# Four quarter-array products in place of four half-array products in one gate of a graph GRU

## The chip, the cores and the metric

The kernel runs on one core of a Trainium2 chip. The metric is the device time of one execution in microseconds (us), as a median over runs. A core has five engines that run their own queues of instructions side by side and wait for one another by semaphores: TensorE (PE in the profile; its weight loads are listed as PEld), VectorE (DVE), ScalarE (ACT), GpSimd (POOL) and SyncE (SP), which here only issues DMA transfers. TensorE reads its operands from SBUF, the on-chip memory of 128 partitions, and writes sums into PSUM, which has eight banks; VectorE and ScalarE read them from there.

## The reference, cut to what matters

There are N = 3327 nodes with 64 features and a dense weighted adjacency matrix `adj` in f32, symmetric in its zeros but not in its weights. Four layers are added to `x`, each on a normalised copy `h`:

```python
def _ggc(x, adj, W, wih, whh, bih, bhh):          # one GRU cell over the graph
    m = adj @ (x @ W)
    gi = m @ wih.T + bih
    gh = x @ whh.T + bhh
    i_r, i_z, i_n = jnp.split(gi, 3, axis=-1)
    h_r, h_z, h_n = jnp.split(gh, 3, axis=-1)
    r = jax.nn.sigmoid(i_r + h_r)
    z = jax.nn.sigmoid(i_z + h_z)
    n = jnp.tanh(i_n + r * h_n)                   # the new value
    return (1.0 - z) * n + z * x

h = relu(layernorm(x));  x = x + relu(_ggc(relu(_ggc(h, ...W1...)), ...W2...))   # layer 0: two cells
# layer 1: adj's non-zeros, ranked and weighted by powers of 1/2, times h @ weight
# layer 2: three products with adj * adj and linear layers;  layer 3: two products with adj, tanh
```

In the gates r and z the input's and the state's sums are only ever needed added together. In the new value n they are needed apart: `h_n` (the state's sum) is first multiplied by r, and then `i_n` (the input's sum) is added.

## The kernel before, in words

**Data.** The nodes are padded to 26 blocks of 128, in two halves of 13 blocks, `s` = 0 and 1. A chunk is a run of 3 or 4 blocks taken from both halves at once: chunks 0, 1 and 2 have 3 blocks (384 columns), chunk 3 has 4 (512 columns). `GROUPS` pairs them: chunks 0 and 1 are group 0, chunks 2 and 3 group 1.

**Products with adj.** There are eight of them, k = 0 to 7; k = 0 and 1 belong to the two GRU cells, k = 2 to the ranked layer. Line L697 (`propagate`) issues them: for a source block and a chunk, one product for each half `s`, each with 128 rows and 64 columns of the array, the first on the left half of the columns and the second on the right half. Their result for a chunk lies in one PSUM bank, half 0 in partitions 0 to 63 and half 1 in partitions 64 to 127. All other products of the kernel have the same 128-by-64 form, and where an operand has only 64 rows, its other half is filled with zeros.

**The GRU cell.** When the sums of a chunk are complete, `after_0` or `after_1` runs `gru`. Its input lies in `both[c]`, 128 partitions by two halves: for each half `s`, the chunk's state is in one half of the partitions and the sums (L942 by ScalarE, then L946 by VectorE in the second cell) are copied into the other. The tile `cells[:, cell, s, g, :]` holds the weights of gate g: g = 0 and 1 are r and z with the input's and the state's weights on top of each other, g = 2 has the state's weights of n in one half of the rows and zeros in the other, g = 3 the input's weights of n in the opposite half of the rows. So `gate(g)` (L1007) is two products, one for each `s`, and gates 2 and 3 multiply 64 of their 128 rows by zeros. In the first cell gate 2 is done ahead of time (`ahead_of_cell`, L217); in the second cell all four gates follow one another. Then ScalarE takes the sigmoids of r and z (L1012), VectorE forms (`nh` + bias) * r (L1017) and adds `ni` (L1019), ScalarE takes the tanh (L1028), and VectorE finishes the cell (L1032 to L1034).

**Order.** Everything is put into the engines' queues in an order fixed at build time. `run` goes through a list of units (one source block for one chunk), and after each unit `spend` advances the tasks that the `yield` statements cut into pieces, by an estimated time. `take` and `give` hand out the eight PSUM banks (`sum` 0 to 3, `temp` 0 to 3). Each engine then works off its own queue, held up only by semaphores.

**What lies around the change.** The second cell runs for chunk 2 at 149.5 us, for chunk 3 at 160.4, for chunk 0 at 200.5 and for chunk 1 at 206.0 (starts of the first gate). Between these VectorE makes masks for the later layers (L509 and L512 for counting, L517 for the ranked layer). From chunk 0's cell on, products of the ranked layer are mixed in: L326 multiplies a mask by a triangular matrix, L575 (ScalarE) or L573 (VectorE) turns the sums into weights, and L697 uses them.

Of the kernel before, what the change touches and what calls it, by code (L numbers as in the profile page):

```python
# [96 lines left out]
def upper(n):  # L97
    return slice(n * D, (n + 1) * D)
# [3 lines left out]
def kernel(  # L102
# [9 lines left out]
    nc = tc.nc  # L112
# [16 lines left out]
    cells = const.tile([P, 2, 2, 4, D], F32, name="cells")  # L129
# [3 lines left out]
    both = [const.tile([P, 2, (b1 - b0) * P], F32, name=f"both{c}") for c, (b0, b1) in enumerate(CH[:NC])]  # L133
# [184 lines left out]
    def width(c):  # L318
        return blocks(c) * P
# [15 lines left out]
    def take(sums=False, either=True):  # L335


        either = either and not sums
        pool = idle_sums if sums else idle_temps
        if either and idle_sums and (not pool or released[idle_sums[0]] < released[pool[0]]):  # L340
            pool = idle_sums
        for c in list(tasks):
            if not pool and c not in running:
                advance(c)
        i = pool.popleft()
        return i, banks[i]

    def give(i):
        released[i] = max(released) + 1
        (idle_sums if i < 4 else idle_temps).append(i)  # L350

    def nodes(c):

        return feat.tile([P, blocks(c), 2, D], F32, name=f"y{c}")
# [17 lines left out]
    def advance(c):  # L372
        running.add(c)
        try:
            tasks[c][1] = next(tasks[c][0])
        except StopIteration:
            del tasks[c]
        running.discard(c)
# [562 lines left out]
    def evacuate_stacked(acc, c, on_scalar=False):  # L941
        nc.scalar.copy(both[c][upper(0), 0], acc[0][1][upper(0), :width(c)])  # L942
        if on_scalar:
            nc.scalar.copy(both[c][upper(1), 1], acc[1][1][upper(1), :width(c)])
        else:
            nc.vector.tensor_copy(both[c][upper(1), 1], acc[1][1][upper(1), :width(c)])  # L946
        for i in {acc[0][0], acc[1][0]}:
            give(i)
# [39 lines left out]
    def turn(yk, c, s):  # L988

        v = both[c][upper(1 - s), s].rearrange("p (b q n) -> p b q n", q=4, n=32)  # L990
        for f in range(2):
            for q in range(4):
                nc.vector.transpose(yk[q * 32:(q + 1) * 32, :, s, f * 32:(f + 1) * 32], v[f * 32:(f + 1) * 32, :, q])

    def gru(acc, c, bi, bh, cell, pace=1.0):

        assert cell in have
        w = width(c)
        evacuate_stacked(acc, c, on_scalar=cell == 0)
        yield 0.8 * pace  # L1000
        at = dead.popleft()
        r, z, d = (slots[at].rearrange("p s w -> p (s w)")[:, i * CWM:i * CWM + w] for i in range(3))

        def gate(g):
            i, ps = take()
            for s in range(2):
                nc.tensor.matmul(ps[upper(1 - s), :w], cells[:, cell, s, g, :], both[c][:, s], start=True, stop=True)  # L1007
            return i, ps

        for g, v in enumerate((r, z)):  # L1010
            i, ps = gate(g)
            nc.scalar.activation(v, ps[:, :w], AF.Sigmoid, bias=bsum[:, cell, g:g + 1])  # L1012
            give(i)
        nh = None if cell == 0 else gate(2)
        ni = gate(3)
        yield 0.75 * pace
        nc.vector.scalar_tensor_tensor(r, ahead[c] if nh is None else nh[1][:, :w], bcol[:, bh + 2:bh + 3], r,  # L1017
                                       op0=ALU.add, op1=ALU.mult)
        nc.vector.tensor_tensor(r, r, ni[1][:, :w], ALU.add)  # L1019
        give(ni[0])  # L1020
        if nh is not None:
            give(nh[0])
        else:
            del ahead[c]
            if not any(ch in ahead for ch in GROUPS[c // 2]):
                rooms[c // 2].free()
        yield 1.2 * pace
        nc.scalar.activation(r, r, AF.Tanh, bias=bcol[:, bi + 2:bi + 3])  # L1028
        yield 0.8 * pace
        for s in range(2):  # L1030
            u = upper(1 - s)
            nc.vector.tensor_tensor(d[u], both[c][u, s], r[u], ALU.subtract)  # L1032
        nc.vector.tensor_tensor(d, d, z, ALU.mult)
        nc.vector.tensor_tensor(d, d, r, ALU.add)  # L1034
        if cell == 0:
            nc.vector.tensor_scalar(both[c][upper(0), 1], d[upper(0)], 0.0, None, op0=ALU.max)
            if c in GROUPS[1]:
                turned[c] = nodes(c)
                turn(turned[c], c, 1)
        yield 2.4 * pace  # L1040
        if cell == 0:
            nc.scalar.activation(both[c][upper(1), 0], d[upper(1)], AF.Relu)
            yield 0.6 * pace
        return at, d
# [27 lines left out]
    def after_0(c, acc):  # L1072
        at, _ = yield from gru(acc, c, BI1, BH1, 0)
        dead.append(at)
        if c in GROUPS[0]:
            yk = nodes(c)
            i, v = stacked_to_nodes(c, lambda s: ident[:, upper(1 - s)])
            yield 0.96
            nc.vector.tensor_copy(flat(yk), v)
            give(i)  # L1080
        else:
            yk = turned.pop(c)
            turn(yk, c, 0)
        y[1][c] = yk

    def after_1(c, acc):
        pace = 1.0 if c in GROUPS[0] else 0.9
        at, h2T = yield from gru(acc, c, BI2, BH2, 1, pace)
        v = transpose_to_nodes(h2T, c)
        dead.append(at)  # L1090
        yield 2.05 * pace
        residual(v, c, relu=True)
        yk = nodes(c)
        yield from layernorm_relu(yk, c, TWO27, 1.2 * pace, squares_on_scalar=c in GROUPS[1])
        y[2][c] = yield from in_three(yk, c)
        yield 80.0 if c in GROUPS[1] else 14.0
        assert "row" in have
        add_row(c, 3)
# [127 lines left out]
```

## Time and profile before

| | |
|---|---|
| median of 3 runs | 685.08 us (684.77 to 685.13) |
| profiled execution | 684.89 us |
| its span in the trace | 683.2 us |
| granted TensorE clock | 1.0 throughout |
| TensorE products issued | 4984 passes, 672.1 us busy |
| VectorE, ScalarE busy | 390.5 us, 272.4 us |
| DMA from the adjacency matrix | 199.08 MB, mean 295 GB/s over the span |

The profile is of one execution. Its span begins with the first and ends with the last recorded instruction, so 1.7 us of the execution's own time lie outside it. An f32 product appears as two TensorE records, one for each of two passes, and each pass has a weight load of its own. The end of a TensorE record is modelled and includes the pipe behind the array, so consecutive records overlap; the distance from one start to the next is what a pass costs in a stream. "128*64" in a row stands for 128 rows and 64 columns of the array. A time in square brackets is how long the engine was idle before that row, with the instruction that released it.

### The profile page before, as it was taken

The page shows a single profiled execution, that of the slowest core. Times are in us where ns is not written, and L with a number is a line of the kernel's source. Part 1 is how long each engine was busy: PE and PEld are TensorE (multiplying, and loading weights), DVE is VectorE, ACT ScalarE, POOL GpSimd, SP SyncE. Part 2 cuts the span into 40 slices and gives each one's busy share as a digit, 9 for nine tenths or more (in the row PEclk, how much of TensorE's full clock was granted, in tenths as well). Part 3 has the DMA queues.
Part 4 walks back from the last instruction along what each step waited for, and adds up shares of the span by engine and source line. Part 5 has one row for each costly group of instructions (what it writes and reads, how often), then busy time and mean ns, then how long its engine had stood idle before and what let it go on. Part 6 is the DMA issues. An engine that isn't in the chain of part 4 may idle for free.

```text
span 683.2 us, 12502 instructions
## 1 busy us (share of the span) xinstructions
PE 672.1 (98%) x4984; PEld 369.8 (54%) x4984; DVE 390.5 (57%) x839; ACT 272.4 (40%) x427; POOL 76.9 (11%) x115
## 2 busy tenths in 40 slices
PE   7999999999999999999999999999999999999997
PEld 5776444445558886566455554444444443344464
DVE  7954898739998999666542108215483893005101
ACT  1014000312148988999987009522366510000101
POOL 5400000002660504021000000000010000000000
PEclk9999999999999999999999999999999999999999
DMA  9999998299889615783999379954997399918991
GB/s 340 401 401 405 405 405 308 78 344 399 279 270 339 244 56 164 274 307 119 358 400 324 124 281 406 406 231 141 401 375 252 123 408 404 405 46 313 397 404 45
DMA packets 68693, 201.30 MB, mean 295 GB/s; under 512 B 7244, under 2 KB 8372, under 8 KB 68636
## 3 DMA queue, kind: packets, MB, share of 16 engines
q1 hardware_dynamic: 65724, 199.08, 78.0%
q10 hardware_dynamic: 736, 1.23, 0.5%
q8 instruction: 39, 0.64, 0.4%
q0 software_dynamic: 2176, 0.20, 0.2%
q14 instruction: 18, 0.15, 0.1%
HBM read 199.45 MB, written 0.85 MB: 293 GB/s over the span
## 4 chain that ended last, share of the span: by engine, by line
PE 94%; DVE 2%; POOL 2%; issue 0%; DMA 0%; ACT 0%; DVEq 0%; ACTq 0%; POOLq 0%
PE sum L697 81%; PE temp L326 5%; PE temp L1007 2%; PE sum L326 1%; PE temp L598 1%; PE sum L1007 1%; PE temp L886 1%; PE temp L611 1%; POOL both L256 1%; DVE e L573 0%; POOL st L966 0%; DMA xs<-in_x 0%; DVE adj L517 0%; DVE st L963 0%; DVE y L962 0%
## 5 line engine op out<-in xcount | busy, mean ns | idle before, releaser
L697 PE MATMUL sum<-adj,y 128*64 128x384 f32 (+3 forms) x3016 | 533.0, 501 | 0.0
L697 PEld LDWEIGHTS sum<-adj,y 128*64 128x64 f32 x3016 | 242.7, 137 | 241.4 <-issue 151.3
L481 ACT ACTIVATE adj<-adj 128x768 f32<-128x768 f32 (+1 forms) x169 | 138.1, 890 | 27.0 <-DMA adj<-in_adjT 13.7
L517 DVE TENSOR_SCALAR adj<-adj 128x768 f16<-128x768 f32 (+2 forms) x156 | 86.2, 594 | 9.8 <-DMA adj<-in_adjT 6.7
L697 PE MATMUL sum<-e,both 128*64 128x384 bf16 (+1 forms) x624 | 73.9, 339 | 0.0
L575 ACT ACTIVATE e<-temp,bitsb 128x384 int16<-128x384 f32 (+1 forms) x113 | 63.6, 605 | 13.2 <-PE temp L326 11.3
L942 ACT COPY both<-sum 64x384 f32<-64x384 f32 (+3 forms) x17 | 8.1, 478 | 145.4 <-PE sum L697 145.3
L483 DVE TENSOR_TENSOR adj<-adj 128x768 f32<-128x768 f32 (+1 forms) x39 | 37.7, 1013 | 42.9 <-DMA adj<-in_adjT 31.8
L946 DVE COPY both<-sum 64x384 f32<-64x384 f32 (+3 forms) x11 | 6.2, 561 | 97.9 <-ACT both L942 96.7
L937 DVE STREAM_TRANSPOSE y<-t 32x96 f32<-32x96 f32 (+1 forms) x128 | 35.6, 278 | 40.8 <-ACT t L922 39.2
L966 POOL TENSOR_TENSOR st<-st,mhalf 128x6 f32<-128x6 f32 (+1 forms) x16 | 25.5, 1592 | 296.9 <-DVE st L964 296.9
L697 PEld LDWEIGHTS <-both 128*64 128x64 bf16 x624 | 44.6, 110 | 13.3 <-issue 3.5
L523 POOL DMA_DIRECT2D adj<-totals x52 | 32.0, 617 | 165.4 <-DVE adj L512 128.6
L326 PE MATMUL temp<-adj,tri 128*64 128x384 bf16 (+1 forms) x316 | 49.0, 341 | 0.1
L573 DVE TENSOR_SCALAR e<-temp 128x384 int16<-128x384 f32 (+1 forms) x45 | 27.7, 618 | 19.1 <-ACT e L575 12.0
L326 PEld LDWEIGHTS <-tri 128*64 128x64 bf16 x416 | 30.3, 110 | 13.7 <-issue 7.8
L915 DVE STREAM_TRANSPOSE both<-y 32x96 f32<-32x96 f32 (+1 forms) x128 | 35.6, 278 | 2.5
L512 DVE SCALAR_TENSOR_TENSOR adj<-adj,adj 128x896 f16<-128x896 f32 x26 | 28.4, 1092 | 0.9
L922 ACT ACTIVATE t<-sum,hopcol 128x384 f32<-128x384 f32 (+1 forms) x8 | 4.9, 608 | 51.8 <-PE sum L697 49.0
L575 ACT ACTIVATE e<-sum,bitsb 128x384 int16<-128x384 f32 (+1 forms) x35 | 20.5, 593 | 5.4 <-PE sum L326 3.8
L598 PE MATMUL temp<-adj,behind 128*64 128x384 f16 x104 | 18.4, 327 | 2.1 <-DVE adj L517 1.9
L326 PE MATMUL sum<-adj,tri 128*64 128x384 bf16 (+1 forms) x100 | 18.5, 335 | 0.9 <-DVE e L573 0.7
(153 smaller groups left out, 360.0 us busy)
## 6 DMA issues: line engine op xcount, KB each, us to landing
adj<-in_adjT SPq DMA_DIRECT2D x130, 768.0 KB, 8.7
adj<-in_adjT SPq DMA_DIRECT2D x104, 896.0 KB, 12.9
xs<-in_x ACTq DMA_DIRECT2D x1, 448.0 KB
adj<-totals POOLq DMA_DIRECT2D x26, 3.0 KB, 4.6
adj<-totals POOLq DMA_DIRECT2D x26, 3.5 KB, 2.9
out<-xs ACTq DMA_DIRECT2D x1, 256.0 KB
xs<-in_x ACTq DMA_DIRECT2D x1, 192.0 KB, 3.1
xs<-in_x SPq DMA_DIRECT2D x1, 192.0 KB
```

Of the source, the lines that this page charges most:

```text
L326: nc.tensor.matmul(out[hs], lhsT[:, hs], rhs, start=start, stop=stop)
L481: nc.scalar.activation(sq, v, AF.Square)
L483: nc.vector.tensor_tensor(sq, v, v, ALU.mult)
L512: nc.vector.scalar_tensor_tensor(t.mask.ones, t.view()[:, 1], 0.0, t.mask.ones, op0=ALU.not_equal, op1=ALU.add)
L517: nc.vector.tensor_scalar(to[:rows, half], t.view()[:rows, half], 0.0, None, op0=ALU.not_equal)
L523: nc.gpsimd.dma_start(out=t.mask.view[P - 1:P], in_=totals[t.g][t.q:t.q + D + 1:D, :])
L573: nc.vector.tensor_scalar(wide[:, s], ps[:, :w], BITS, 0.0, op0=ALU.add, op1=ALU.max)
L575: nc.scalar.activation(wide[:, s], ps[:, :w], AF.Relu, bias=bitsb)
L697: nc.tensor.matmul(acc[h][1][h * D:(h + 1) * D, :w], yq[h], rhs[h], start=first and n == 0, stop=last and n == len(terms) - 1)
L915: nc.vector.transpose(to[at:at + 32, :, q], h[q * 32:(q + 1) * 32, :, s, f * 32:(f + 1) * 32])
L937: nc.vector.transpose(yk[q * 32:(q + 1) * 32, :, s, f * 32:(f + 1) * 32], v[at:at + 32, :, q])
L966: nc.gpsimd.tensor_tensor(st[:, 3, :n], st[:, 2, :n], mhalf[:, :n], ALU.pow)
```

## The change

In the second cell, gates 2 and 3 are no longer two calls of `gate`. Both PSUM banks are taken first, and then four products are issued, each with only the 64 rows that hold weights. For each half `s` of the nodes one product is the state's, into the bank `nh`, and one the input's, into `ni`. The two use opposite halves of the rows and the same half of the columns, so that the four products lie in the four quarters of the array. The zeros are not multiplied any more. The first cell keeps its form; only its two lines are written differently.

```diff
             i, ps = gate(g)
             nc.scalar.activation(v, ps[:, :w], AF.Sigmoid, bias=bsum[:, cell, g:g + 1])
             give(i)
-        nh = None if cell == 0 else gate(2)
-        ni = gate(3)
+        if cell == 0:
+            nh, ni = None, gate(3)
+        else:
+            nh, ni = take(), take()
+            for s in range(2):
+                for (_, ps), g, rows in ((nh, 2, upper(1 - s)), (ni, 3, upper(s))):
+                    nc.tensor.matmul(ps[upper(1 - s), :w], cells[rows, cell, s, g, :], both[c][rows, s],
+                                     start=True, stop=True)
         yield 0.75 * pace
```

`upper(n)` is the slice of partitions from 64 n to 64 n + 63. The issue order before was: state's sum for `s` = 0, state's for `s` = 1, input's for 0, input's for 1. It is now: state's for 0, input's for 0, state's for 1, input's for 1. The banks, the number of products, passes and weight loads, and the order on all other engines stay as they were; the wait for the bank of `ni` moves from the third product to the second.

## The prediction

> **What bounds the kernel now.** I read the page first: its busy times and the chain that ended last.
>
> ```profile
> PE 672.1 (98%) x4984; PEld 369.8 (54%) x4984; DVE 390.5 (57%) x839; ACT 272.4 (40%) x427; POOL 76.9 (11%) x115
> ...
> PE 94%; DVE 2%; POOL 2%; issue 0%; DMA 0%; ACT 0%; DVEq 0%; ACTq 0%; POOLq 0%
> ```
>
> TensorE is busy for 98% of the span and holds 94% of the chain, so over the whole kernel its time is the end. But the change sits in four places only, the second cell's gates of chunks 2, 3, 0 and 1 (near 150, 161, 201 and 207 us), and there the question is which wait ends last. So next came the gate line L1007 and the timeline of weight loads at chunk 0.
>
> ```profile
> L1007 PE MATMUL temp<-both,cells x72: 486/486/592, 60.8 to 208.3; 128*64 128x384 f32 x56, 128*64 128x512 f32 x16
> ```
>
> ```profile
> 200.52 0.20 PEld L1007 LDWEIGHTS sum<-both,cells 128*64 128x64 f32 x4 [0.62 <-DVE both L946]
> 200.90 0.14 PEld L1007 LDWEIGHTS temp<-both,cells 128*64 128x64 f32 x2 [0.18 <-ACT e L575]
> ...
> 201.87 0.14 PEld L1007 LDWEIGHTS temp<-both,cells 128*64 128x64 f32 x2 [0.18 <-issue]
> 202.19 0.14 PEld L1007 LDWEIGHTS temp<-both,cells 128*64 128x64 f32 x2 [0.18 <-ACT adj L1012]
> 202.51 0.14 PEld L1007 LDWEIGHTS temp<-both,cells 128*64 128x64 f32 x2 [0.18 <-issue]
> ```
>
> Each f32 product is two passes, and the two halves of the columns run side by side: a pair of weight loads every 0.32 us. A pass of 384 columns thus costs 0.322 us of stream, though its record says 0.486: the other 0.164 us is the pipe behind it, which the next pass covers. A product of 384 columns is 0.645 us, one of 512 columns 0.86 us (the chain gives 0.86 us to its four passes). The gates begin at 200.52 because they waited for VectorE's copy at L946. That sent me to VectorE.
>
> ```profile
> 152.40 0.62 DVE L1017 SCALAR_TENSOR_TENSOR adj<-sum,bcol,adj 128x384 f32<-128x384 f32 x1 [2.31 <-PE sum L1007]
> ...
> 153.83 0.63 DVE L509 TENSOR_SCALAR adj<-adj 128x896 f16<-128x896 f32 x1 [0.16 <-PE sum L697]
> ```
>
> ```profile
> 159.69 0.69 DVE L946 COPY both<-sum 64x512 f32<-64x512 f32 x1 [0.25 <-ACT both L942]
> ```
>
> ```profile
> 199.91 0.56 DVE L946 COPY both<-sum 64x384 f32<-64x384 f32 x1
> ...
> 202.81 0.62 DVE L1017 SCALAR_TENSOR_TENSOR adj<-temp,bcol,adj 128x384 f32<-128x384 f32 x1 [1.28 <-PE temp L1007]
> ```
>
> ```profile
> 159.70:200.40 40.70, 40.70 (x316) 23.63 (x312) 39.94 (x83) 9.41 (x20) 25.34 (x37) 1.00 0.88 305
> ```
>
> The last line is a stretch with busy times of TensorE, weight loads, VectorE, ScalarE and GpSimd: VectorE works 39.94 of 40.70 us. From 159.69 to 201.53 it waits for nobody, and between 152.40 and 159.69 it has only two short waits (0.16 and 0.25 us). TensorE and VectorE are tied here within tenths of a microsecond.
>
> **Part 1, what is removed.** Four products of 128 rows, two on each half of the columns one after the other, become four of 64 rows, which can run side by side. Pass and load counts stay. If they do run side by side, one product time goes per chunk: 3 x 0.645 + 0.86 = 2.79 us, 0.41% of the time. That is the ceiling.
>
> **Part 2, what is added: two changes of the array's division per chunk**, into quarters and back. Every TensorE row of before is 128*64, so no row shows one. From below: nothing (a change from fp16 to f32 operands, L634 to L697 at 199.73, leaves no gap), and not below nothing, since no pass gets shorter by it. From above: the pipe empties and the weights load in the open, 0.164 + 0.05 = 0.21 us; the 0.05 is what the restart at 200.52 lost (0.37 us to the next pass instead of 0.32). I take 0.21, since a restart from an empty pipe is the row that it is nearest to. Net gain on TensorE: 0.645 - 0.43 = 0.215 us in a chunk of 384 columns, 0.43 in chunk 3.
>
> The Trainium skill says in TensorEngine Tiling (Array Packing), Key Properties, that changing the tiling mode drains TensorE; it gives no price, and no run here shows one yet. By that rule the sum is the one with 0.21 us; without it, the one of the first rival.
>
> **Part 3, when VectorE gets its operands.** L1017 reads the state's sum (`nh`). In the new order its second half is the third product, which now starts with the others: it ends one change, 0.21 us, later than before. The input's sum (`ni`) is ready some 0.4 us earlier, but L1019 runs after L1017 and never waited for it.
>
> **Part 4, what reaches the end.** Chunk 2: L1017 starts 0.21 us later, and the wait of 0.16 us at L509 shrinks by about 0.12, so VectorE is free at 159.53 instead of 159.44. The accumulator is done 0.215 us earlier, so ScalarE's L942 ends at 159.45 instead of 159.66. L946 moves from 159.69 to about 159.55. Chunk 3: the gates start some 0.1 us earlier, `nh` comes 0.21 us later than that, so L1017 (163.36 before) starts 0 to 0.1 us later. From there VectorE is packed to 200.47, so chunk 0's gates start where they did, at 200.5: what TensorE gained in chunks 2 and 3 (0.65 us) becomes idle time before L946.
>
> Chunk 0: 0.215 us, and this passes on. L326 after the gates comes earlier, ScalarE's L575 follows (it was idle 0.9 us before), then L942 and L946 of chunk 1, and VectorE has 1.0 us free before that L946 (204.98 to 206.00), which covers the later L1017. Chunk 1: 0.215 us again; what follows (L575 at 209.68, the tanh at L1028, L573 at 212.22) is released by TensorE, with ScalarE 0.9 us idle before. The other edits cost nothing: the `ni` bank is claimed 0.645 us earlier, but the only waiting one, chunk 0's, hangs on ScalarE's L635, which ends at 201.52, before the quarters begin at 201.87.
>
> Sum: 684.89 (span 683.2 and 1.7 around it) - 0.43 = 684.46 for the profiled execution, which lies 0.19 below the median of 685.08. So 684.6 as a median, 0.07% faster. About 0.2% (1.37 us) is what a measurement of this kernel can tell from no change, so this reads as the same. With changes of 0.05 to 0.35 us each, this case runs from 683.7 to 685.4.
>
> **Rival 1, free changes.** If the array re-divides between two passes, each chunk keeps 0.645 us. VectorE is then not delayed at L1017, and gives back about 0.36 us of its two short waits, which also reaches chunk 0: 0.36 + 2 x 0.645 = 1.65, so 683.4. For it: the change of operand type costs nothing. Against: nothing shows rows re-divided. Even here the gain of chunk 3 is lost in the packed VectorE.
>
> **Rival 2, slower: the row halves take turns.** Nothing in the trace shows two products sharing a half of the columns at once. If they take turns, nothing is removed and both changes are paid: 0.43 us lost per chunk. Chunk 2 then delays L946 by 0.43; chunk 3's `nh` comes 0.43 + 0.21 late, so packed VectorE brings chunk 0 some 0.7 us late, and chunks 0 and 1 add 0.43 each: 1.55 us, 686.6. With side-by-side quarters TensorE itself loses from 0.32 us per change; changes of 0.5 us, no row of which I have, would give 1.4 us or more the same way, by late `nh` (a small case, 686.5 and up).
>
> **Rival 3, slower: products start strictly in program order.** Then a product's second pass holds back the next one's first, and four products take five passes, 1.61 + 0.43 against 1.29 us: 0.75 lost, 0.86 in chunk 3. `nh` is late by 0.86 and 1.07, VectorE brings 1.8 us to chunk 0, two times 0.75 follow: 3.3 us, 688.4. The timeline at chunk 2 speaks against it:
>
> ```profile
> 151.53 0.49 PE L1007 MATMUL temp<-both,cells 128*64 128x384 f32 x1
> ...
> 151.81 0.49 PE L1007 MATMUL sum<-both,cells 128*64 128x384 f32 x1
> ```
>
> There sum is gate 2 and temp gate 3. A pass of gate 3 starts at 151.53, ahead of gate 2's last at 151.81, on the other half of the columns. So halves are not held to one order; that quarters aren't either is a step beyond. The Trainium skill, in TensorE: Matmul & The Clock Gate, part 3, says that matmuls start and end strictly in order; by that rule it would be this rival, and the two rows disagree with it.
>
> **How the numbers follow.** Side by side with paid changes 0.50 (684.6); free changes 0.20 (683.4); turns 0.17 (686.6); dear changes 0.06; program order 0.07 (688.4). Faster by over 0.2% is the second case, 0.20; same the first, 0.50; slower the other three, 0.30. The range goes from 683.2, just below the free case, to 687.0, above the turns; it leaves out program order and the dearest changes.
>
> **What would show it.** In the trace after, the four quarters' first passes at chunk 0 should start within some 0.05 us of each other, about 0.2 us after the last pass of gate 1 has left its stream, and the next line's first pass about 1.07 us after that stream's end instead of 1.29. VectorE's wait at L1017 of chunk 2 should grow by 0.2 us, and TensorE's wait for L946 at chunk 0 by some 0.6 us. It is wrong if pass starts in the quarters are 0.32 us apart, if chunk 0's gates start more than 0.3 us away from 200.5, or if a wait appears that isn't at these four places.

## The result and the profile after

| | before | changed |
|---|---|---|
| median of 18 runs each, us | 684.97 (684.69 to 685.23) | 683.76 (683.62 to 684.35) |
| profiled execution, us | 684.89 | 683.78 |
| its span, us | 683.2 | 682.1 |

The ratio is 0.9983 (0.9977 to 0.999): 1.21 us or 0.17% faster. That is still inside the 0.2% taken as the bound of "the same", but the interval lies wholly below 1. The new median lies between the forecast (684.6) and the first rival (683.4).

The page of the changed kernel, busy times and chain:

```profile
PE 670.8 (98%) x4984; PEld 363.7 (53%) x4984; DVE 389.4 (57%) x839; ACT 272.4 (40%) x427; POOL 77.7 (11%) x115
...
PE 93%; DVE 3%; POOL 2%; issue 1%; ACT 0%; DMA 0%; DVEq 0%; ACTq 0%; POOLq 0%
```

The numbers of instructions are those of before; TensorE's busy time fell by 1.3 us. The quarters are line L1020. This row has its 20 passes into the `temp` banks; 12 more, of the same form, go into `sum` banks:

```profile
L1020 PE MATMUL temp<-both,cells x20: 482/533/640, 151.7 to 207.7; 64*64 64x384 f32 x16, 64*64 64x512 f32 x4
```

**Do the quarters run side by side?** The timeline of TensorE's passes at chunk 2, in the changed kernel:

```profile
151.71 0.53 PE L1020 MATMUL sum<-both,cells 64*64 64x384 f32 x1
151.72 0.53 PE L1020 MATMUL temp<-both,cells 64*64 64x384 f32 x1
151.72 0.53 PE L1020 MATMUL sum<-both,cells 64*64 64x384 f32 x1
151.73 0.53 PE L1020 MATMUL temp<-both,cells 64*64 64x384 f32 x1
152.08 0.48 PE L1020 MATMUL sum<-both,cells 64*64 64x384 f32 x1
152.09 0.48 PE L1020 MATMUL temp<-both,cells 64*64 64x384 f32 x1
```

Yes: four products start their first passes within 0.02 us, and their second passes follow 0.37 us later, again together.

**What does a change of the division cost?** The same engine at chunk 0:

```profile
200.81 0.81 PE L1007 MATMUL temp<-both,cells 128*64 128x384 f32 x4
201.55 0.88 PE L1020 MATMUL temp<-both,cells 64*64 64x384 f32 x8
202.36 0.35 PE L326 MATMUL temp<-adj,tri 128*64 128x384 bf16 x2
202.54 0.33 PE L326 MATMUL sum<-adj,tri 128*64 128x384 bf16 x2
```

Gate 1's records end at 201.62; without the pipe of 0.164 us its stream ends at 201.456. The quarters begin at 201.55, so 0.09 us later, and their first pass takes 0.37 us instead of 0.322, since its weights load in the open: 0.14 us. On the way back, the stream ends at 202.43 - 0.164 = 202.266, L326 begins at 202.36, again 0.09 us later, and the first pair is 0.02 us longer than the next (0.35 against 0.33; 0.05 us where the next line is f32, as at chunk 2). So a change costs 0.11 to 0.14 us, not 0.21. From gate 1's stream to the next line it is 0.90 us, where before had 1.29 and the prediction 1.07. With the 0.02 us of the longer first pair, 1.29 - 0.92 = 0.37 us is what TensorE saves in this chunk.

**Who waits for it?** VectorE in the changed kernel, in three stretches of its timeline (L1023 is what was L1017, L1025 was L1019):

```profile
152.71 0.62 DVE L1023 SCALAR_TENSOR_TENSOR adj<-sum,bcol,adj 128x384 f32<-128x384 f32 x1 [2.48 <-PE temp L1020]
...
153.90 0.62 DVE L509 TENSOR_SCALAR adj<-adj 128x896 f16<-128x896 f32 x1
...
158.55 1.09 DVE L512 SCALAR_TENSOR_TENSOR adj<-adj,adj 128x896 f16<-128x896 f32 x1
159.67 0.69 DVE L946 COPY both<-sum 64x512 f32<-64x512 f32 x1
```

```profile
163.58 0.75 DVE L1023 SCALAR_TENSOR_TENSOR adj<-temp,bcol,adj 128x512 f32<-128x512 f32 x1 [0.18 <-PE sum L1020]
164.44 0.69 DVE L1025 TENSOR_TENSOR adj<-adj,sum 128x512 f32<-128x512 f32 x1
165.04 1.96 DVE L517 TENSOR_SCALAR adj<-adj 127x768 bf16<-127x768 f32 x4
```

```profile
199.50 0.56 DVE L946 COPY both<-sum 64x384 f32<-64x384 f32 x1
...
202.56 0.62 DVE L1023 SCALAR_TENSOR_TENSOR adj<-temp,bcol,adj 128x384 f32<-128x384 f32 x1 [1.44 <-PE temp L1020]
...
205.22 0.56 DVE L946 COPY both<-sum 64x384 f32<-64x384 f32 x1 [0.92 <-ACT both L942]
```

Up to 149 us the two traces agree but for a constant: each instruction of the changed kernel stands 0.14 us later against the start of its span. That constant is taken off in all that follows (for the other kernels it is -0.12 to 0.11 us). The starts on VectorE then move by these amounts, in us against before:

| VectorE's instruction | changed | group 0 only | group 1 only | chunk 3 only | zeroing off GpSimd (else as before) | changed, zeroing twice |
|---|---|---|---|---|---|---|
| L1017, chunk 2 (152.40) | +0.17 | 0 | +0.17 | 0 | 0 | +0.17 |
| L946 for chunk 3 (159.69) | -0.17 | 0 | -0.16 | 0 | 0 | -0.16 |
| L1017, chunk 3 (163.36) | +0.08 | 0 | +0.09 | +0.18 | 0 | +0.09 |
| L1032, chunk 3 (167.39) | -0.50 | 0 | -0.50 | -0.41 | -0.59 | +0.15 |
| L946 for chunk 0 (199.91) | -0.55 | -0.05 | -0.48 | -0.42 | -0.18 | +0.16 |
| L946 for chunk 1 (206.00) | -0.92 | -0.42 | -0.48 | -0.42 | -0.18 | -0.21 |
| near 250 us | -1.28 | -0.78 | -0.47 | -0.41 | -0.18 | -0.57 |

The first column tells the story. Chunks 0 and 1 give 0.37 and 0.36 us, one after the other, down to the last two rows. Chunk 2's gain comes to nothing: at chunk 3 VectorE is 0.08 us late. But between 163.58 and 167.39 VectorE gets 0.6 us faster, in a stretch that the prediction had taken as fixed. The two groups of rows there are, in the kernel before (VectorE, then GpSimd):

```profile
164.82 2.54 DVE L517 TENSOR_SCALAR adj<-adj 127x768 bf16<-127x768 f32 x4
```

```profile
164.81 0.73 POOL L653 MEMSET adj<- 128x768 f32 x1 [2.67 <-PE sum L697]
```

and GpSimd in the changed kernel:

```profile
164.31 0.73 POOL L653 MEMSET adj<- 128x768 f32 x1 [2.19 <-PE sum L697]
```

Four masks of L517 took 2.54 us before and take 1.96 now. Before, the first of them started at 164.82 together with GpSimd's zeroing of a buffer (L653, in `last_sources`) and took 1.14 us instead of 0.55:

```profile
164.82 1.14 DVE L517 TENSOR_SCALAR adj<-adj 127x768 bf16<-127x768 f32 x1
```

The zeroing waits for TensorE (the product L697 that last read the buffer). Chunk 3's gates are now shorter, so it is released 0.64 us earlier and is over at 165.04, just when L517 starts. The kernel before has such a collision once more: L517 at 204.00 takes 0.98 us beside the zeroing of group 1's buffer (203.73, 0.84 us). That one is gone in the changed kernel too (0.55 us at 203.75), but VectorE had 1.02 us free behind it, so it had cost nothing.

The two stretches from chunk 3's L1017 to chunk 0's L946, before and changed (span, then busy times of TensorE, weight loads, VectorE, ScalarE, GpSimd):

```profile
163.36:199.91 36.55, 36.55 (x294) 21.81 (x292) 35.96 (x77) 7.55 (x17) 22.89 (x33) 1.00 0.87 295
```

```profile
163.58:199.50 35.92, 35.92 (x290) 20.33 (x288) 35.32 (x76) 7.50 (x17) 23.63 (x33) 1.00 0.90 303
```

VectorE is packed in both, as the prediction said, but the pack is 0.63 us shorter. That TensorE needs less time in this stretch too (its chunk 3 saves 0.86 - 2 x 0.14 = 0.58 us) is what lets the early copy be of use. The sum is 0.55 (chunk 3 with the collision gone) + 0.37 + 0.36 = 1.28 us. The medians differ by 1.21 us, and the two profiled executions by 1.11, since the constant of 0.14 us goes the other way.

So the theory for the experiments was: changes cost 0.14 us; chunks 0 and 1 pass all of it on; of group 1 only chunk 3 counts, and only since the zeroing no longer meets L517. The rival: the gain of group 1 is TensorE's own, and VectorE's faster stretch is a by-product.

### The profile page after: what moved, and what is told of

Its sections match the earlier page's. It is cut to its first block, busy times and chain, and to the rows that moved or that the text cites. A ratio compares the mean times of both kernels' runs of the same rounds, so it can differ in the third digit from the quotient of the medians.

```text
span 682.1 us, 12502 instructions
## 1 busy us (share of the span) xinstructions
PE 670.8 (98%) x4984; PEld 363.7 (53%) x4984; DVE 389.4 (57%) x839; ACT 272.4 (40%) x427; POOL 77.7 (11%) x115
## 4 chain that ended last, share of the span: by engine, by line
PE 93%; DVE 3%; POOL 2%; issue 1%; ACT 0%; DMA 0%; DVEq 0%; ACTq 0%; POOLq 0%
PE sum L697 80%; PE temp L326 5%; PE temp L1007 2%; PE sum L326 1%; PE temp L598 1%; PE temp L886 1%; PE sum L1007 1%; PE temp L611 1%; POOL both L256 1%; DVE e L573 0%; DMA xs<-in_x 0%; POOL st L966 0%; PE temp L1020 0%; DVE adj L517 0%; DVE st L963 0%
## 5 line engine op out<-in xcount | busy, mean ns | idle before, releaser
L697 PE MATMUL sum<-adj,y 128*64 128x384 f32 (+3 forms) x3016 | 532.4, 501 | 0.0
L697 PEld LDWEIGHTS sum<-adj,y 128*64 128x64 f32 x3016 | 240.8, 137 | 243.5 <-issue 161.8
L517 DVE TENSOR_SCALAR adj<-adj 128x768 f16<-128x768 f32 (+2 forms) x156 | 85.1, 588 | 9.5 <-PE temp L598 4.8
L697 PE MATMUL sum<-e,both 128*64 128x384 bf16 (+1 forms) x624 | 72.5, 339 | 0.0
L946 DVE COPY both<-sum 64x384 f32<-64x384 f32 (+3 forms) x11 | 6.2, 561 | 97.6 <-ACT both L942 96.4
L697 PEld LDWEIGHTS <-both 128*64 128x64 bf16 x624 | 42.8, 110 | 14.5 <-issue 3.5
L326 PE MATMUL temp<-adj,tri 128*64 128x384 bf16 (+1 forms) x316 | 47.4, 341 | 0.1
L326 PEld LDWEIGHTS <-tri 128*64 128x64 bf16 x416 | 28.7, 110 | 14.8 <-issue 8.2
L512 DVE SCALAR_TENSOR_TENSOR adj<-adj,adj 128x896 f16<-128x896 f32 x26 | 28.4, 1092 | 0.9
L326 PE MATMUL sum<-adj,tri 128*64 128x384 bf16 (+1 forms) x100 | 17.4, 336 | 0.9 <-DVE e L573 0.7
```

The costliest lines, as they stand in the source:

```text
L326: nc.tensor.matmul(out[hs], lhsT[:, hs], rhs, start=start, stop=stop)
L512: nc.vector.scalar_tensor_tensor(t.mask.ones, t.view()[:, 1], 0.0, t.mask.ones, op0=ALU.not_equal, op1=ALU.add)
L517: nc.vector.tensor_scalar(to[:rows, half], t.view()[:rows, half], 0.0, None, op0=ALU.not_equal)
L697: nc.tensor.matmul(acc[h][1][h * D:(h + 1) * D, :w], yq[h], rhs[h], start=first and n == 0, stop=last and n == len(terms) - 1)
```

## The experiments

### Quarters in chunks 0 and 1 only

```diff
+        elif not (c in GROUPS[0]):
+            nh, ni = gate(2), gate(3)
         else:
```

> Quarters in chunks 0 and 1 only; chunks 2 and 3 as before. Theory S (gated): each visit to the quarters takes 0.37 us off TensorE, in chunks 0 and 1 this reaches the end, and nothing of it comes from before 200 us: 0.74 us faster than before, 684.2. VectorE's L517 near 164.8 still takes 1.14 us, and L946 of chunk 0 starts where it did in the kernel before. Theory R (every chunk counts, and the whole change in time is TensorE's): also 0.74 us, or 0.55 if the measured 1.2 us is shared out by columns.

Measured: 684.27 us, ratio to before 0.9989 (0.998 to 0.9997), so 0.77 us faster. In the table, L946 for chunk 0 hardly moves (-0.05), and the two chunks then give 0.37 and 0.36 us. L517 at chunk 3 still collides, as in before:

```profile
164.70 2.54 DVE L517 TENSOR_SCALAR adj<-adj 127x768 bf16<-127x768 f32 x4
```

Chunks 0 and 1 are thus worth what TensorE saves there: 2 x 0.37.

### Quarters in chunks 2 and 3 only

```diff
+        elif not (c in GROUPS[1]):
+            nh, ni = gate(2), gate(3)
         else:
```

> Quarters in chunks 2 and 3 only; chunks 0 and 1 as before. Theory S: TensorE gains 0.95 us in the two chunks, but chunk 0's gates wait for VectorE's L946, which comes only 0.45 to 0.55 us earlier, since the L517 near 165 takes 0.55 us instead of 1.14 (GpSimd's zeroing L653 runs before it and not beside it): 0.5 us faster than before, 684.5. Theory R: all 0.95 us, 684.0.

Measured: 684.50 us, 0.9993 (0.9984 to 1.0002), 0.54 us less by the medians. The interval touches no change, so the trace has to say it: L517's four masks take 1.96 us, L946 for chunk 0 comes 0.48 us earlier, and that stays to the end (-0.47). With the 0.77 of the other group it adds up to 1.31, the whole change having 1.21.

### Quarters in chunk 3 only

```diff
+        elif not (c == 3):
+            nh, ni = gate(2), gate(3)
         else:
```

> Quarters in chunk 3 only. Theory S (gated by VectorE, and the zeroing moves with TensorE): TensorE comes out of chunk 3's gates 0.5 to 0.6 us earlier, GpSimd's zeroing L653, which TensorE releases, goes with it and misses the L517 (0.55 us instead of 1.14), so both engines reach chunk 0 about 0.45 us earlier: 684.55, nearly all that chunks 2 and 3 brought together (684.50). If chunk 2 had its own share in it: 684.8. If the zeroing alone made the gain: 684.9, as with ScalarE's zeroing.

Measured: 684.51 us, 0.9994 (0.9985 to 1.0003): the same as with chunk 2 beside it. L946 for chunk 0 comes 0.42 us earlier here and 0.48 there. Chunk 2's quarters save about 0.3 us on TensorE (the next L611 begins at 159.27 instead of 159.42, and the constant comes on top) and bring at most 0.06 of it. Where the rest goes is seen in the changed kernel's weight loads after chunk 2:

```profile
159.69 0.11 PEld L611 LDWEIGHTS <-behind 128*64 128x64 f16 x1 [0.31 <-issue]
...
160.23 0.46 PEld L1007 LDWEIGHTS temp<-both,cells 128*64 128x64 f32 x4 [0.18 <-issue]
```

The counting product L611 takes the mask that VectorE's L512 makes (158.55 + 1.09 = 159.64 us). Its last load is put down to "issue", but it comes 0.05 us after L512's end, and L512 itself is 0.06 us later than in before, because L1023 started late. TensorE, ahead after chunk 2, stands still here until VectorE has caught up, and chunk 3's gates start 0.06 us earlier instead of 0.3.

### The collision taken out of the kernel before

The zeroing of group 0's buffer goes from GpSimd to ScalarE, in the kernel before; nothing else is changed.

```diff
-        nc.gpsimd.memset(v, 0.0)
+        if g == 0:
+            nc.scalar.activation(v, xs.rearrange("p b s d -> p (b s d)")[:, :w], AF.Copy, scale=0.0)
+        else:
+            nc.gpsimd.memset(v, 0.0)
```

> The kernel before, with the zeroing L653 of group 0 done by ScalarE (a copy scaled by 0) and not by GpSimd; no quarters. Theory S: the L517 near 164.8 takes 0.55 us instead of 1.14, VectorE comes to chunk 0's L946 0.5 to 0.6 us earlier, and TensorE is next late after 0.1 to 0.2 us: 0.15 us faster than before, 684.85. Theory R: L517's length is a bystander (or is set by something else): no change of the time, and if L517 stays at 1.14 us, GpSimd is not its cause.

Measured: 684.91 us, 0.9999 (0.9991 to 1.0008), no difference that can be told. The trace shows why. VectorE's timeline in this kernel:

```profile
164.91 1.96 DVE L517 TENSOR_SCALAR adj<-adj 127x768 bf16<-127x768 f32 x4
...
199.83 0.56 DVE L949 COPY both<-sum 64x384 f32<-64x384 f32 x1 [0.42 <-ACT both L945]
```

L517 is back at 1.96 us, with no zeroing on GpSimd beside it, so the collision was the cause of the 0.58 us. But at the copy before chunk 0 VectorE now stands idle for 0.42 us and waits for ScalarE's copy, which waits for the sums of TensorE. Of VectorE's 0.59 us only 0.18 arrives there. With VectorE alone shortened, TensorE is the next in line, 0.18 us behind.

### The zeroing started earlier, in the changed kernel

```diff
+        if g == 0:
+            nc.gpsimd.memset(v[:, :w // 2], 0.0)
         nc.gpsimd.memset(v, 0.0)
```

> The changed kernel, with half of the zeroing L653 of group 0 done once more ahead of it on GpSimd (0.37 us), so that it runs later and again beside the L517 that follows chunk 3's L1025. Theory S: that L517 takes 0.3 to 0.6 us longer, VectorE's L946 of chunk 0 comes as much later, and the kernel is 0.3 to 0.6 us slower than the changed one: 684.1 to 684.4. Theory R: as the changed kernel, 683.8.

Measured: 683.90 us, 0.9984 (0.9975 to 0.9993). The run doesn't decide anything: the added half ran early, at 162.10, where its part of the buffer was already free, and the whole zeroing still began at 164.34, as in the changed kernel. It didn't reach L517, which took as long as without it. The next one puts the load where it was meant to be.

### The collision put back into the changed kernel

The zeroing of group 0's buffer is done twice over, so that GpSimd is still at it when L517 starts.

```diff
-        nc.gpsimd.memset(v, 0.0)
+        for _ in range(2 if g == 0 else 1):
+            nc.gpsimd.memset(v, 0.0)
```

> The changed kernel, with the whole zeroing L653 of group 0 done twice on GpSimd, so that the second one runs near 165.0 to 165.8 us. Theory S: the first L517 after chunk 3's L1025 takes about 1.1 us instead of 0.55, VectorE's L946 of chunk 0 comes 0.5 to 0.6 us later, and the kernel is 0.4 to 0.6 us slower than the changed one: 684.2 to 684.4. Theory R (the zeroing is a bystander): 683.8.

Measured: 684.50 us, 0.9994 (0.9985 to 1.0002), 0.74 us above the changed kernel's 683.76. VectorE and GpSimd in this kernel:

```profile
165.00 2.61 DVE L517 TENSOR_SCALAR adj<-adj 127x768 bf16<-127x768 f32 x4
```

```profile
164.27 1.53 POOL L654 MEMSET adj<- 128x768 f32 x2 [2.19 <-PE sum L698]
```

The four masks take 0.65 us more than in the changed kernel, L946 for chunk 0 comes 0.71 us later, and near 250 us it is still 0.71. TensorE has the same products and quarters as in the changed kernel, so the rival (the gain of group 1 is TensorE's own) is refuted. Together with the run that takes the collision out of the kernel before: the 0.55 us need both, TensorE ahead and VectorE free of the collision. With the collision the change gives chunks 2 and 3 nothing, which is what the prediction had for them; L946 for chunk 0 even comes 0.16 us later than in before.

### Products of 64 rows with no one to share with

The two products of the state's sum are moved between gates 0 and 1, and the input's follow after gate 1. Each pair lies on opposite halves of the columns, so nothing shares a half, and the array's division is changed four times a chunk instead of twice.

```diff
+        def halves(g, flip):
+            i, ps = take()
+            for s in range(2):
+                rows = upper(1 - s if flip else s)
+                nc.tensor.matmul(ps[upper(1 - s), :w], cells[rows, cell, s, g, :], both[c][rows, s],
+                                 start=True, stop=True)
+            return i, ps
...
+            if g == 0 and cell == 1:
+                nh = halves(2, True)
+        ni = gate(3) if cell == 0 else halves(3, False)
```

> The second cell in all four chunks with products of 64 rows, but the state's pair is issued between gates 0 and 1 and the input's pair after gate 1, so that no two products share a half of the columns and the array's division changes four times per chunk. Theory S (the gain comes from sharing alone and each change costs 0.14 us): TensorE loses 0.58 us per chunk; with VectorE's waits for the late input's sum some 1 us by chunk 0 and 0.58 twice after it: 2 to 2.3 us slower than before, 687.1. Rival (products of 64 rows are cheaper in themselves, or changes are free once their loads are queued): as before or faster, 685.0 or less.

Measured: 687.13 us, 1.0031 (1.0019 to 1.0043), 2.17 us slower. The weight loads of this kernel at chunk 0 (L1014 is the 64-row pair):

```profile
201.55 0.20 PEld L1007 LDWEIGHTS sum<-both,cells 128*64 128x64 f32 x4 [0.50 <-DVE both L946]
202.35 0.19 PEld L1014 LDWEIGHTS temp<-both,cells 64*64 64x64 f32 x4 [0.60 <-ACT totals L635]
203.14 0.20 PEld L1007 LDWEIGHTS temp<-both,cells 128*64 128x64 f32 x4 [0.60 <-ACT totals L635]
203.94 0.20 PEld L1014 LDWEIGHTS temp<-both,cells 64*64 64x64 f32 x4 [0.60 <-issue]
204.73 0.14 PEld L326 LDWEIGHTS <-tri 128*64 128x64 bf16 x4 [0.60 <-issue]
```

Each step is 0.79 to 0.80 us, where a pair of products streams for 0.645: 0.15 us per change, in four steps one after the other. Sixteen changes make 2.4 us, and the trace shows VectorE 2.37 us late at the end. So a pass of 64 rows is no shorter than one of 128, and all that the change gains comes from the sharing.

### Quarters in both cells

The first cell too forms its state's and input's sums together, in quarters; the products that did the state's sum ahead of time (`ahead_of_cell`) are gone.

```diff
-            ahead_of_cell(c)
...
-        if cell == 0:
-            nh, ni = None, gate(3)
-        else:
-            nh, ni = take(), take()
+        nh, ni = take(), take()
```

> The changed kernel, with the first cell done in the same way: no state's sum ahead of time (L217, its ScalarE copy and its room in SBUF go), four quarters in its gates. Theory S: TensorE gains 0.37 us per chunk of 384 columns and 0.58 in chunk 3 there too; if TensorE alone sets the end near 60 and 120 us, 1.7 us more: 682.1. If the DMA stream or VectorE is as near there as VectorE was in the second cell: 683.4 to 683.8.

Measured: 683.30 us, 0.9975 (0.9966 to 0.9985). That is 1.66 us below before and, by the medians, 0.46 below the changed kernel, the lowest of all that ran. Of this 0.46 the traces show 0.19 near 250 us (the constant, here 0.04, taken off), and the intervals of the two ratios to before overlap. TensorE alone would give 2.79 (the products done ahead) less 8 x 0.14 for the changes, 1.67 us. The stretch ahead of the first cell, in this kernel and in before (columns as above):

```profile
45.00:60.00 15.00, 14.41 (x101) 7.58 (x97) 7.70 (x16) 0.86 (x2) 0.00 (x0) 1.00 1.03 402
```

```profile
45.00:60.00 15.00, 15.00 (x111) 11.49 (x108) 7.84 (x16) 1.54 (x3) 0.00 (x0) 1.00 1.03 402
```

and its waits from 30 to 60.5 us:

```profile
PEld sum L696 <- DMA adj<-in_adjT: 2.4, 5, 0.6
```

TensorE was busy throughout in before and now waits for the matrix, which arrives at 402 GB/s in both kernels; before has no such wait in this window. The sums of the first cell's first chunk are complete 1.1 us earlier instead of 2.8, and eight changes (1.12 us) are then paid for out of that. At the second cell's first VectorE copy, L946 of chunk 2 (here L945), 0.28 us is left (149.29 against 149.53, and the constant). No run here shows in detail how these add up.

## Why the prediction was right and where it was wrong

**Right: what bounds, and how the quarters run.** The first passes start within 0.02 us of each other. Rival 2 (the halves take turns) and rival 3 (program order) are refuted by the same rows, and rival 1 by the timeline at chunk 0, where a change costs something. The rows also bear against the rule of the Trainium skill that rival 3 named (TensorE: Matmul & The Clock Gate, part 3). If a product's two passes stand together in the queue, as one call issues both (no row shows the queue itself), then with order kept strictly the other products' first passes could not start 0.36 us ahead of the first product's second.

**Mis-sized: the price of a change, in part 2.** 0.21 us was taken from a restart out of an empty pipe; 0.14 was measured, and 0.15 in the kernel with four changes. The 0.05 us for the open weight load was right. The other term was not: the quarters begin 0.09 us after the last stream's end, not 0.164, so 0.07 us before gate 1's records end. TensorE thus gains 0.37 us in a chunk of 384 columns instead of 0.215, and 0.58 in chunk 3 instead of 0.43. Chunks 0 and 1 alone bring 0.73 instead of 0.43.

The Trainium skill (TensorEngine Tiling (Array Packing), Key Properties) says that a change of the mode drains TensorE. The gap of 0.09 us at each change agrees with it, though the rows, whose ends are modelled, don't show whether the pipe was empty by then. By that rule a price of more than nothing was to be expected, and the runs add how much.

**Right: chunk 2, part 4.** L1017 starts 0.17 us later (0.21 forecast), L509's wait is gone, L512 ends 0.06 us later (0.09), L946 comes 0.17 us earlier (0.14), chunk 3's gates 0.06 us earlier (0.1), and its L1017 0.08 us later (0 to 0.1). The reason that the prediction gave for chunk 3's gates is not the one, though. L946 is over at 160.36, before they start at 160.52; what holds them back is TensorE's wait at L611 for VectorE's L512, a wait at none of the four places, which the prediction had named as a sign of being wrong.

**Wrong: "From there VectorE is packed to 200.47, so chunk 0's gates start where they did".** VectorE was packed, but not with work of a fixed length: 0.59 us of it was the time that one mask lost beside GpSimd's zeroing, and when the zeroing runs hangs on TensorE. Chunk 0's gates start at 200.11, 0.55 us earlier with the constant taken off, the sign that the prediction named for being wrong; the 0.6 us of idle time before L946 did not appear. This term, taken as 0, is 0.55 us of the 1.28. With the collision put back it is gone, and chunks 2 and 3 give nothing. The trace of before had it to see: four L517 in 2.54 us, where two of them take 1.03 at 160.42.

**Right: chunks 0 and 1 pass on all that TensorE saves**, with VectorE's slack at L946 (0.92 us left of 1.0) as cover. Part of that slack is luck: the second collision, at 204.00, went away as well and gave VectorE 0.43 us back there, which the prediction hadn't seen.

**The numbers.** 0.43 us was forecast: 2 x 0.215. 1.28 came in the trace: 0.30 more by the smaller price in chunks 0 and 1, 0.55 more by the collision, in which the smaller price in chunk 3 is contained. So the forecast had the way and the smallness of the change right, but only a third of the gain. That the time lies nearer to rival 1 (683.4) than to the forecast (684.6) is chance, as changes are not free. It even lies within the bounds of the prediction's main case (683.7 to 685.4), but that is luck too: the lower bound stands for changes of 0.05 us, and with the measured 0.14 us the prediction's own sum gives 0.73 us, some 684.3. The rest is the zeroing, of which it knew nothing.

## What to carry to other kernels

Products that fill only half of the array's rows can share it with their likes. What they bring is the stream time of one product for each pair that shares, less two changes of the division, here up to 0.14 us each. So a product has to stream for longer than both changes together, and the likes have to stand next to each other in the queue: apart from each other they cost 0.15 us per change and bring nothing. Before an engine's packed stretch is taken as fixed, look for an instruction in it that takes longer than its likes, and ask what moves when the other engine gets faster. Where two engines are tied, one of them shortened shows almost nothing, and a run with only one of the two gains says so plainly.

## What the runs showed of the hardware

- Four products of 64 rows and 64 columns run at once, with first passes some 7 ns apart (151.71 to 151.73); a pass takes as long as one of 128 rows. To get in and out costs 0.14 us each way for f32, and less (0.11) when bf16 follows.
- A mask of L517 (f32 to bf16, 127x768) takes 0.55 us, and 1.14 us when GpSimd's zeroing of 128x768 f32 (0.73 us) has just begun. In before the zeroing ends at 164.81 + 0.73 = 165.54 and the mask 0.42 us after that; in the kernel with two zeroings they end at 165.80, and the first mask, 1.21 us long, 0.41 us after. The collision at 204.00 ends the same way: the zeroing at 203.73 + 0.84 = 204.57, the mask 0.41 us after it. So the mask looks stopped until the zeroing is over, not slowed. The kernel with 64-row products apart shows the other order: a mask runs from 165.79 to 166.34 when the zeroing starts at 166.00, and there the zeroing takes 1.02 us instead of 0.73; the next mask takes 1.17 us and again ends 0.41 us after it. L1025, which ran beside the zeroing in the changed kernel, took 0.69 us, as without it.

The Trainium skill says, in SBUF — State Buffer, Who interferes with whom, that VectorE in a two-port mode and GpSimd share a pair of ports, that whoever comes first keeps it for the whole instruction, and that tensor_scalar is among the operations that can use that mode. The rests of 0.41 and 0.42 us agree with it, and so does the zeroing that takes 1.02 us when the mask was first.

- ScalarE's zeroing of the same buffer (165.7 to 166.5, beside the four masks from 164.91 to 166.87) left them at 1.96 us, so it is GpSimd's work and not the write into the buffer that stops VectorE.
